# The second projection of a gated recurrence and a shared feed-forward net: one level of Strassen's form against two

## The chip, the cores and the metric

The kernel runs on one core of one Trainium2 chip. The metric is the device time of one execution in microseconds (us). Three runs of the kernel before gave 4150.46, 4151.88 and 4153.29 us, so a median of 4151.88 us. Everything is in 32-bit floats.

## What is computed

The input x is 8 sequences of 1024 tokens with 512 features. The reference, cut to its core:

```python
xn = layernorm(x)
proj = xn @ W1 + b1                        # 512 -> 3 * 1024: hidden, forget, input
hidden, f, i = split(proj, 3)
h = scan of a gated recurrence over the tokens of a sequence
s = h @ W2 + b2                            # 1024 -> 512
shared = (silu(xn @ sgate) * (xn @ sup)) @ sdown      # 512 -> 1024 -> 512
routed = the same with one of 32 experts per token (arg max of xn @ gate_w)
out = x + s * silu(shared + routed)
```

The change concerns the two products with 1024 rows of weights: h @ W2 and the shared net's product with sdown.

## The kernel before

The 8192 tokens are cut into 16 chunks of 512. The work of a chunk is 20 *jobs*: a job makes 256 columns of one of the five first products (hidden, forget, input, gate, up). Each job is a product in Strassen's form: 7 outer products in place of 8 (`multiply`, matmuls at L918), each of them two matmuls of 128 x 128 weights on 256 columns. The trace shows every float matmul as two records, so such an outer product is four records. The program is written out as *slots*, 7 to a job and 140 to a chunk (`SC`). In each slot there is one outer product of a job; `ORDER` fixes which. Work on other engines is put into the slots with `at(slot, ...)`. Each engine then runs its instructions in the order in which the program issues them; within a slot that is first the outer product and its eviction (L932, L934, on ACT), then the steps put there by `at`, then the fill, of which below.

The evictions of a job are joined by adds (L944) one slot later, on DVE, and one of the seven on POOL. A `Cell` (from L948) turns forget, input and hidden of two blocks of 128 rows into the recurrence: a chain of activations on ACT and of tensor operations on DVE at fixed slots after the job's first slot g, among them the two logarithms at g+29 and g+31 (L992, ACT), the difference at g+32 (L996, DVE), two more at g+33 and g+34 (L1000, L1004), and the scans at g+45 and g+47 (L1029). There are four Cells in a chunk, with g at slots 0, 21, 56 and 91. A `Prep` normalizes the next chunk (`normal`, L619) and asks the router; a few of its results go through the PSUM bank that `work` gives out.

The second products of chunk c run in the slots of chunk c+1, as a *fill*: `project_out` is a generator, and `due` says how many of its steps are to be issued by each slot. A chunk has two *units*, half 0 (h @ W2) in slots 1 to 62 and half 1 (the shared net) in slots 63 to 136. A unit is again one product in Strassen's form: 7 outer products `UNIT`, each of 8 matmuls (L1240) of 128 x 128 on 256 columns; a fill step is one matmul, 56 to a unit. Sums of blocks on the left (`out_combine`, L1183) are made on POOL and DVE beforehand; the right sides, 512 KB each, are read from HBM one outer product at a time by `out_fetch` (L1159 to L1164) into three buffers (`wo`). Two PSUM banks (`ps_u`) hold the outer products; each is read out once, 512 elements a partition (L1220, L1223, L1252, L1258, L1263), and the results go to HBM in two stores (L1204). All these transfers are issued on SP's queue, beside the weights of the jobs (L742), their kept sums (L804) and the traffic of `Prep`.

PSUM's eight banks: three for the jobs' chains (`ps_b`), two for their side products (`ps_x`), two for the fill (`ps_u`), and one for `work`.

After the last chunk's slots (END) the rest of the fill runs alone, and then 32 experts are worked through (L308 to L520) with the tokens gathered by a table that `Dispatch` builds during the last chunks; an expert's products are in Strassen's form too (L398), with 118 to 174 columns to a matmul.

Of the kernel before, what the change touches and what calls it, by code (L numbers as in the profile page):

```python
# [34 lines left out]
def tile_kernel(  # L35
# [73 lines left out]
    def work(name):  # L109
        return pools["work"].tile([P, 512], FP, tag="w", name=name)  # L110
# [16 lines left out]
    def iota(name, n, step, base, cm=0):  # L127
        tf = const.tile([P, n], FP, name=name)

        def fill():  # L130
            ti = const.tile([P, n], I32, name=name + "_i", tag="iota_i")
            nc.gpsimd.iota(ti, pattern=[[step, n]], base=base, channel_multiplier=cm)
            nc.vector.tensor_copy(tf, ti)

        later.append(fill)
        return tf
# [446 lines left out]
    class Prep:  # L583
# [127 lines left out]
        def plan(self, g):  # L711
# [15 lines left out]
            at(g + 66, self.router)  # L727
            at(g + 72, self.logits)
            at(g + 76, self.choose)
# [21 lines left out]
    vrow = const.tile([4 * NJ, P], FP, name="vrow")  # L751
# [5 lines left out]
    def zero_rows():  # L757
# [3 lines left out]
        zrow = op.tile([1, H], FP, tag="ea", name="zrow")  # L761
# [119 lines left out]
    def multiply(name, n):  # L881
# [64 lines left out]
        if name == "P2":  # L946
            evict(part("a", 2), None)
# [8 lines left out]
        elif name == "P7":  # L956
            evict(part("u3", 2), 1)
            join(nc.gpsimd if c else nc.vector, o[:, 1, HT:], "u3", "p5")
        elif name == "P4":
            evict(o[:, 1, :HT], 1)  # L960
            natural.pop(n)
# [6 lines left out]
    class Cell:  # L968
# [53 lines left out]
        def scan(self, s):  # L1022
            c, p = self.c, self.p
            j = 2 * p + s
            if s == 0:
                rnn_h[c, p] = hp.tile([P, 2, T], FP, tag="r", name=f"h{c}_{p}", bufs=5)
# [58 lines left out]
    UNIT = ("P1", "P2", "P6", "P5", "P7", "P3", "P4")  # L1085
# [14 lines left out]
    def out_load(half, k, m):  # L1100

        tag, bufs = (("r", 5), ("s", 6))[half]
# [34 lines left out]
    out_w, out_s = {}, {}  # L1137
    far_turn = iter(range(2 * len(UNIT)))
    out_next = iter([(u, name) for u in units for name in UNIT])

    def out_fetch():

        u, name = next(out_next, (None, None))
        if u is None:
            return
        half = u[1]
        if "far" in pools:
            turn = next(far_turn)
            if turn % 5 < 2:
                o = pools["far"].tile([P, NP, HC], FP, tag="far", name=f"far{turn}")  # L1150
            else:
                o = out_tile(f"w{name}_{half}")
            out_w[u, name] = o
        else:
            o = out_w[u, name] = out_tile(f"w{name}_{half}")
# [9 lines left out]

    HALF = 2 * P
# [5 lines left out]
    def out_combine(c, half, q, p):  # L1172
        if p == 0:
            out_s[q] = op.tile([P, NP, HALF], FP, tag=f"s{q}", name=f"s{q}_{c}_{half}")
        A11, A12, A21, A22 = out_part(c, half, p)
        o = out_s[q][:, p, :]
        eng, l, r, op_ = {
            1: lambda: (nc.gpsimd, A21, A22, ALU.add),
            2: lambda: (nc.vector, out_s[1][:, p, :], A11, ALU.subtract),
            3: lambda: (nc.gpsimd, A11, A21, ALU.subtract),  # L1180
            4: lambda: (nc.vector, A12, out_s[2][:, p, :], ALU.subtract),
# [3 lines left out]
    for c in range(NCHUNK):  # L1185
        g = SC * (c + 1)
        fast = c == NCHUNK - 1
        for p in range(NP):
            for q in range(1, 5):
                if p == NP - 1:  # L1190
                    slot = (1, 2, 4, 6)[q - 1]
                else:
                    slot = (110, 112, 122, 132)[q - 1] + p - SC
                at(g + slot, out_combine, c, 0, q, p)
                if fast:
                    slot = (20, 22, 26, 30)[q - 1] + p // 2
                else:
                    slot = (42, 44, 52, 61)[q - 1] + p
                at(g + slot, out_combine, c, 1, q, p)

    def out_store(c, half, m, o):
        i = (c * NT + 2 * m) * P
        rows = rec2[i : i + 2 * P, half * H : (half + 1) * H]
        nc.sync.dma_start(out=rows.rearrange("(q p) f -> p q f", p=P), in_=o)  # L1204

    def project_out():

        for n, u in enumerate(units):
            c, half = u

            chain, side = (
                ps_u.tile([P, 2, HC], FP, tag=f"u{(n + k) % 2}", name=f"u{k}_{n}")
                for k in range(2)
            )
            o = [op.tile([P, 2, H], FP, tag=f"o{m}", name=f"o{half}_{c}_{m}") for m in range(2)]
            part = {}

            def copy(o, ps, m):
                if half:
                    nc.scalar.copy(o, ps)  # L1220
                else:
                    bias = b2b[:, m * HC : (m + 1) * HC].unsqueeze(1).to_broadcast([P, 2, HC])
                    nc.vector.tensor_tensor(o, ps, bias, ALU.add)  # L1223

            def evict(name, ps, m):
                t = part[name] = op.tile([P, 2, HC], FP, tag="e" + name[0], name=f"{name}_{n}")
                copy(t, ps, m)

            for name in UNIT:
                w = out_w.pop((u, name))  # L1230
                if half:
                    w = w.rearrange("p q (m a r) -> p q a m r", m=KH, r=BL)
                ps = side if name in ("P2", "P5", "P3") else chain
                for q in range(2):
                    for p in range(NP):
                        if name in ("P1", "P2", "P4"):
                            lhs = out_part(c, half, p)[{"P1": 0, "P2": 1, "P4": 3}[name]]
                        else:
                            lhs = out_s[{"P5": 1, "P6": 2, "P7": 3, "P3": 4}[name]][:, p, :]
                        nc.tensor.matmul(  # L1240
                            ps[:, q, :], lhsT=lhs[:, q * P : (q + 1) * P], rhs=w[:, p],

                            start=(q == 0 and p == 0 and name in ("P1", "P2", "P5")),
                            stop=(p == NP - 1),

                            skip_group_check=True,
                        )
                        if q == 1 and p == NP - 1:
                            if name == "P1":
                                evict("a1", ps, 0)  # L1250
                            elif name == "P2":
                                nc.vector.tensor_tensor(o[0][:, :, :HC], ps, part["a1"], ALU.add)  # L1252
                            elif name == "P6":
                                evict("a2", ps, 1)
                            elif name == "P5":
                                evict("b5", ps, 1)
                            elif name == "P7":
                                nc.scalar.copy(o[1][:, :, HC:], ps)  # L1258
                                nc.gpsimd.tensor_tensor(
                                    o[1][:, :, HC:], o[1][:, :, HC:], part["b5"], ALU.add  # L1260
                                )
                            elif name == "P3":
                                nc.vector.tensor_tensor(o[0][:, :, HC:], ps, part["a2"], ALU.add)  # L1263
                                at(now + 2, out_store, c, half, 0, o[0])
                            else:
                                copy(o[1][:, :, :HC], ps, 0)
                                at(now + 2, out_store, c, half, 1, o[1])
                            out_fetch()
                        yield

    class Dispatch:
# [16 lines left out]
        def ranks(self, q):  # L1288
# [22 lines left out]
            for _ in range(9):  # L1311
                yield
            ps = work(f"bef{q}")
# [492 lines left out]
```

## Time and profile before

The profiled execution took 4152.99 us; its span from the first to the last instruction is 4151.0 us. Busy time of the engines by stretches of the span:

| stretch, us | what runs | PE | ACT | DVE | POOL | DMA share | GB/s |
|---|---|---|---|---|---|---|---|
| 0 to 163 | chunk 0's jobs, no fill | 134.78 | 103.65 | 111.96 | 85.71 | 0.76 | 252 |
| 163 to 334 | jobs of chunk 1, fill of chunk 0 | 171.00 | 113.14 | 96.36 | 32.38 | 0.72 | 231 |
| 334 to 2564 | jobs of chunks 2 to 14, fill of chunks 1 to 13 | 2230.00 | 1476.17 | 1206.31 | 448.79 | 0.67 | 214 |
| 2564 to 2734 | jobs of chunk 15, fill of chunk 14 | 168.85 | 112.82 | 90.10 | 102.20 | 0.60 | 183 |
| 2734 to 2790 | fill of chunk 15 | 54.63 | 7.46 | 24.92 | 15.69 | 0.77 | 256 |
| 2790 to 4151 | the experts | 1339.84 | 300.79 | 725.95 | 707.73 | 0.77 | 225 |

PE is the matrix engine TensorE, ACT ScalarE, DVE VectorE, POOL GpSimd, SP SyncE. A column of an engine is the time in which it was busy; the DMA share is the mean busy share of the 16 DMA engines. Matmuls overlap, so a record's duration (379 ns for 256 columns) is longer than the distance from its start to the next one's, which is what a stream of matmuls costs. The granted clock of PE is 0.997 of full speed over the whole span.

### The profile page before, as it was taken

Reading aid. Unit: us, or ns where it says so; the run is one execution under the profiler, and the core shown is the slowest. Engines: PE = TensorE matmul, PEld = TensorE weight load, DVE = VectorE, ACT = ScalarE, POOL = GpSimd, SP = SyncE. Lnnn points to the kernel's source line nnn. Section 1 sums busy time; section 2 is a strip of 40 time slices with the busy share of each in tenths; the row PEclk is TensorE's granted clock in tenths of the full one; section 3 lists DMA queues with packets and bytes.
Section 4 is the critical chain, followed back from the end, with each engine's and each line's share of the span. In section 5 each row is a group of like instructions: output and inputs, shape, how many; then the busy total and the mean of one; then the engine's idle time right before and its main releaser. Section 6 shows DMA issues by size and latency. Waiting matters only on the chain. (4 is left out here: it accounts for less than half of the span.)

```text
span 4151.0 us, 60142 instructions
## 1 busy us (share of the span) xinstructions
PE 4099.1 (99%) x21515; PEld 3634.4 (88%) x21515; DVE 2255.6 (54%) x3682; ACT 2114.0 (51%) x4031; POOL 1392.5 (34%) x1539
## 2 busy tenths in 40 slices
PE   7999999999999999999999999999999999999997
PEld 5788888888888888888888888887899999999997
DVE  6655555564555645556455566534555656666631
ACT  5666666666666667666676666731222222222210
POOL 5322111221112211212112122634555555555542
PEclk9999999999999999999999999999999999999999
DMA  8776666666666766667666665666778787887884
GB/s 277 238 221 221 210 221 204 216 224 212 219 206 213 228 214 218 211 198 229 220 218 214 202 223 180 186 221 199 211 228 233 220 244 231 247 252 233 244 262 116
DMA packets 557537, 909.30 MB, mean 219 GB/s; under 512 B 55404, under 2 KB 315404, under 8 KB 556980
## 3 DMA queue, kind: packets, MB, share of 16 engines
q1 hardware_dynamic: 508228, 812.03, 60.9%
q0 software_dynamic: 46880, 89.20, 8.9%
q8 instruction: 172, 2.82, 0.3%
q10 hardware_dynamic: 2128, 4.19, 0.3%
q14 instruction: 129, 1.06, 0.1%
HBM read 786.82 MB, written 136.37 MB: 222 GB/s over the span
## 5 line engine op out<-in xcount | busy, mean ns | idle before, releaser
L918 PE MATMUL b<-t,sums 128*128 128x256 f32 x2536 | 653.9, 380 | 13.3 <-ACT u L932 6.9
L1240 PE MATMUL u<-wP,s 128*128 128x256 f32 x2032 | 596.1, 379 | 0.6 <-ACT a L1220 0.6
L918 PEld LDWEIGHTS b<-t,sums 128*128 128x128 f32 x2536 | 480.8, 190 | 83.1 <-ACT u L932 8.5
L332 PE MATMUL acc<-e_h,e_wd 128*128 128x284 f32 (+26 forms) x2048 | 514.7, 394 | 0.0
L1240 PEld LDWEIGHTS u<-wP,s 128*128 128x128 f32 x2032 | 385.7, 190 | 55.0 <-issue 1.9
L332 PEld LDWEIGHTS acc<-e_h,e_wd 128*128 128x128 f32 x2048 | 373.6, 190 | 64.9
L918 PE MATMUL b<-t,nat 128*128 128x256 f32 x1268 | 325.9, 379 | 5.5 <-ACT u L932 4.7
L253 POOL DMA_INDIRECT e_xs<-rec,fours x276 | 300.2, 1088 | 91.1 <-issue 87.4
L918 PE MATMUL a<-xnT,nat 128*128 128x256 f32 x1268 | 326.3, 380 | 0.0
L918 PE MATMUL c<-xnT,sums 128*128 128x256 f32 x1268 | 325.6, 379 | 0.0
L918 PE MATMUL b<-xnT,nat 128*128 128x256 f32 x1268 | 325.4, 379 | 0.0
L918 PE MATMUL c<-t,sums 128*128 128x256 f32 x1268 | 325.4, 379 | 0.0
L934 ACT ACTIVATE u<-b,vec 128x256 f32<-128x256 f32 x378 | 179.8, 476 | 188.0 <-PE b L918 171.9
L918 PEld LDWEIGHTS b<-t,nat 128*128 128x128 f32 x1268 | 240.5, 190 | 40.0 <-ACT u L932 6.3
L918 PEld LDWEIGHTS a<-xnT,nat 128*128 128x128 f32 x1268 | 241.4, 190 | 33.0
L918 PEld LDWEIGHTS c<-xnT,sums 128*128 128x128 f32 x1268 | 241.3, 190 | 33.0
L918 PEld LDWEIGHTS b<-xnT,nat 128*128 128x128 f32 x1268 | 240.9, 190 | 33.2 <-issue 0.5
L918 PEld LDWEIGHTS c<-t,sums 128*128 128x128 f32 x1268 | 240.9, 190 | 32.8
L1240 PE MATMUL u<-wP,h 128*128 128x256 f32 x768 | 225.2, 379 | 0.0
L996 DVE TENSOR_TENSOR d<-d,m 128x1024 f32<-128x1024 f32 x64 | 87.7, 1370 | 239.8 <-ACT m L992 239.8
L1240 PE MATMUL u<-wP,sh 128*128 128x256 f32 x720 | 215.6, 381 | 0.0
L407 ACT COPY e_s<-e_b 128x284 f32<-128x284 f32 (+21 forms) x216 | 84.4, 391 | 238.6 <-PE e_b L398 238.6
(291 smaller groups left out, 7794.1 us busy)
## 6 DMA issues: line engine op xcount, KB each, us to landing
sums<-sdram SPq DMA_DIRECT2D x300, 512.0 KB, 4.8
nat<-in_L_attn_W_dram SPq DMA_DIRECT2D x192, 512.0 KB, 4.7
wP<-tdram SPq DMA_DIRECT2D x127, 512.0 KB, 4.0
e_w<-L_ffn_routed_gate_w_dram SPq DMA_DIRECT2D x126, 512.0 KB, 4.6
e_w<-n_L_ffn_routed_up_w_dram SPq DMA_DIRECT2D x126, 512.0 KB, 8.1
e_wd<-L_ffn_routed_down_w_dram SPq DMA_DIRECT2D x31, 2048.0 KB, 11.0
nat<-L_ffn_shared_gate_w_dram SPq DMA_DIRECT2D x64, 512.0 KB, 4.9
nat<-n_L_ffn_shared_up_w_dram SPq DMA_DIRECT2D x64, 512.0 KB, 4.4
```

Of the source, the lines that this page charges most:

```text
L253: nc.gpsimd.indirect_dma_start(out=self.xs[t][:, b, :], out_offset=None, in_=rec1.rearrange("n (a d) -> (n a) d", a=NA), in_offset=bass.In ...
L332: nc.tensor.matmul(accs[m][:, :W], lhsT=self.wd[:, j, m * P : (m + 1) * P], rhs=h[:, :W], start=(j == 0), stop=(j == NI - 1),)
L407: nc.scalar.copy(o[:, :W], ps[:, :W])
L918: nc.tensor.matmul(ps, lhsT=lhs[:, k, :], rhs=rhs[:, k, :], start=(new and k == 0), stop=(k == KQ - 1),  skip_group_check=True,)
L934: nc.scalar.activation(o, ps, AF.Identity, bias=bias(n, block))
L996: nc.vector.tensor_tensor(d, d, self.li, ALU.subtract)
L1240: nc.tensor.matmul(ps[:, q, :], lhsT=lhs[:, q * P : (q + 1) * P], rhs=w[:, p],  start=(q == 0 and p == 0 and name in ("P1", "P2", "P5")), ...
```

## The change

For chunks 1 to 14 (`deep`) each of the 7 outer products of a unit is itself made in Strassen's form: 7 inner products (`INNER`) of two matmuls each, 128 x 128 on 128 columns, where there were 8 matmuls on 256 columns. A fill step is now one inner product, 49 to a unit. Inner product i of outer product b stands at step 7b + 3i, so that three outer products are in work at any time, each in a PSUM bank of its own; the third bank is the one that `work` had, and `work` now borrows a bank of `ps_x` in the last slot of a job, to which its users are moved (`aligned`, the router's slots). In a bank, inner P1, P6, P7 and P4 follow each other in the first 128 columns, P2 has the next 128, and P5 and P3 the third.

Four inner products are copied out (ACT, or DVE where the bias is added), three are added to such a copy on DVE one slot later; when an outer product is complete, `out_add` sums the outer products on DVE. The sums of inner blocks on the left are made on POOL (`inner_sum`). The right sides of the inner products are made once, in chunk 0's units, which still run with one level: POOL makes the four sums of an outer product (`out_make`), ACT copies three raw blocks (`out_raw`), and both are written to HBM in pieces of 128 KB. From then on the pieces are read back, four to a buffer, one inner product to a piece.

The order of `UNIT`, the slots of `out_combine`, and some buffers change with it: the jobs' eviction tiles a and u3 have one buffer in place of two, h has four in place of five, results are stored in four quarters of a unit, and some tiles at the start share a buffer. Chunks 0 and 15 keep one level.

```diff
     def work(name):
-        return pools["work"].tile([P, 512], FP, tag="w", name=name)
+        if now < SC:
+            return pools["work"].tile([P, 512], FP, tag="w", name=name)
+        assert now % 7 == 6
+        return ps_x.tile([P, 512], FP, tag=f"x{(now // 7 + 1) % 2}", name=name)
+
+    def aligned():
+        while now % 7 != 6:
+            yield
...
-            at(g + 66, self.router)
-            at(g + 72, self.logits)
-            at(g + 76, self.choose)
+            at(g + 69, self.router)
+            at(g + 76, self.logits)
+            at(g + 77, self.choose)
...
-            evict(part("a", 2), None)
+            evict(part("a", 1), None)
...
-            evict(part("u3", 2), 1)
+            evict(part("u3", 1), 1)
...
-                rnn_h[c, p] = hp.tile([P, 2, T], FP, tag="r", name=f"h{c}_{p}", bufs=5)
+                rnn_h[c, p] = hp.tile([P, 2, T], FP, tag="r", name=f"h{c}_{p}", bufs=4)
...
+    HQ = HC // 2
+    UNIT = ("P1", "P2", "P4", "P6", "P5", "P3", "P7")
+    INNER = ("P1", "P2", "P5", "P6", "P3", "P7", "P4")
...
+    ALL = [(c, half, name) for c, half in units for name in UNIT]
+
+    def deep(b):
+        return 0 < ALL[b][0] < NCHUNK - 1
+
+    LAST = max(b for b in range(len(ALL)) if deep(b))
+    inner_of = {}
+    for b in range(len(ALL)):
+        if deep(b):
+            for i, name in enumerate(INNER):
+                inner_of[7 * b + 3 * i] = (b, name)
...
+    FAR = 3
...
+    def groups(piece):
+        piece = [s for s in piece if s in inner_of]
+        for k in range(0, len(piece), 4):
+            yield ("pieces", piece[k : k + 4])
...
+        if kind == "pieces":
+            o = o.rearrange("p q f -> p (q f)").rearrange("p (s f) -> p s f", s=4)
+            for k, step in enumerate(what):
+                b, name = inner_of[step]
+                out_w[step] = o[:, k, :].rearrange("p (q f) -> p q f", q=2)
+                nc.sync.dma_start(
+                    out=o[:, k, :], in_=tdram2[ALL[b][1:]][:, INNER.index(name), :]
+                )
+            return
...
+        for o, l, r in (
+            (t[:, 0], B12, B11), (t[:, 1], B22, t[:, 0]), (t[:, 3], B21, t[:, 1]),
+            (t[:, 2], B22, B12),
+        ):
+            nc.gpsimd.tensor_tensor(o, l, r, ALU.subtract)
...
+        for k, i in enumerate(("P5", "P6", "P7", "P4")):
+            nc.sync.dma_start(out=d[:, INNER.index(i), :], in_=made[:, k, :])
...
+            r = jp.tile([P, 2, KH, BL], FP, tag=f"i{i[1]}", name=f"raw{b}{i}", bufs=1)
+            nc.scalar.copy(r, quarter(w, half, k, n))
+            at(now + 2, lambda r=r, i=i: nc.sync.dma_start(
+                out=tdram2[half, name][:, INNER.index(i), :], in_=r.rearrange("p q m r -> p (q m r)"),
+            ))
...
-                if p == NP - 1:
-                    slot = (1, 2, 4, 6)[q - 1]
-                else:
-                    slot = (110, 112, 122, 132)[q - 1] + p - SC
+                ends = p == NP - 1
+                slot = {
+                    1: 1 if ends else 134 + p - SC, 2: 2 if ends else 137 + p - SC,
+                    4: 8 + p, 3: 13 + p // 2 if fast else 18 + p,
+                }[q]
                 at(g + slot, out_combine, c, 0, q, p)
                 if fast:
-                    slot = (20, 22, 26, 30)[q - 1] + p // 2
+                    slot = (24, 26, 31, 28)[q - 1] + p // 2
                 else:
-                    slot = (42, 44, 52, 61)[q - 1] + p
+                    slot = (62, 66, 82, 72)[q - 1] + p
...
+        if half or name not in ("P2", "P4", "P5"):
+            nc.scalar.copy(o, ps)
+            return
+        first += HC * (name == "P5")
+        bias = b2b[:, first : first + n]
+        if reps:
+            bias = bias.unsqueeze(1).to_broadcast([P, reps, n])
+        nc.vector.tensor_tensor(o, ps, bias, ALU.add)
...
+    def out_bank_of(b):
+        n = b % 3
+        if n == 2:
+            return pools["work"].tile([P, 512], FP, tag="w", name=f"u{b}")
+        return ps_u.tile([P, 2, HC], FP, tag=f"u{n}", name=f"u{b}").rearrange("p q f -> p (q f)")
...
+        if name == "P2":
+            add(o(0, 0), R)
+            at(now + 2, out_store, b, 0, 0)
+        elif name == "P6":
+            add(R, out_r[b])
+        elif name == "P3":
+            add(o(0, 1), o(1, 1))
+            add(o(0, 1), R)
+            at(now + 2, out_store, b, 0, 1)
+        elif name == "P7":
+            add(R, out_r[b])
+            for n in (1, 0):
+                add(o(1, n), R)
+                at(now + 2, out_store, b, 1, n)
...
+    def inner_sum(b, q):
+
+        o = inner[b, q] = jp.tile([P, 2, P], FP, tag=f"i{q}", name=f"i{q}_{b}", bufs=1)
+        A11, A12, A21, A22 = (inner_block(b, m, k) for m in range(2) for k in range(2))
...
+        l, r, what = {
+            1: lambda: (A21, A22, ALU.add), 2: lambda: (made(1), A11, ALU.subtract),
+            3: lambda: (A11, A21, ALU.subtract), 4: lambda: (A12, made(2), ALU.subtract),
+        }[q]()
+        for o, l, r in zip(parts, l, r):
+            nc.gpsimd.tensor_tensor(o, l, r, what)
...
+        b, name = inner_of[step]
+        if name == "P1":
+            out_bank[b] = out_bank_of(b)
+        n = {"P2": 1, "P5": 2, "P3": 2}.get(name, 0)
+        ps = out_bank[b][:, n * P : (n + 1) * P]
+        w = out_w.pop(step)
+        for i, lhs in enumerate(inner_lhs(b, name)):
+            nc.tensor.matmul(
+                ps, lhsT=lhs, rhs=w[:, i, :], start=(name == "P1" and i == 0), stop=(i == 1),
+                skip_group_check=True,
+            )
+        o = {"P2": (0, 0), "P3": (0, 1), "P4": (1, 0), "P7": (1, 1)}.get(name)
+        o = o and target(b)[:, o[0], o[1] * HQ : (o[1] + 1) * HQ]
+        side = {"P2": "P1", "P3": "P6", "P7": "P5"}.get(name)
+        if side:
+            kept = inner.pop((b, side))
+            at(now + 1, lambda: nc.vector.tensor_tensor(o, ps, kept, ALU.add))
+        elif name == "P4":
+            out_copy(b, o, ps, 0, HQ)
+            at(now + 2, out_add, b)
+        else:
+            e = inner[b, name] = jp.tile(
+                [P, HQ], FP, tag="e" + name, name=f"e{name}_{b}", bufs=1 + (name == "P5")
+            )
+            out_copy(b, e, ps, 0 if name == "P1" else HQ, HQ)
...
+        def step(s):
+            if s in inner_of:
+                inner_product(s)
+                used[0] += 1
+                if used[0] % 4 == 0 or s == left[-1]:
+                    out_fetch()
+
+        for b, (c, half, name) in enumerate(ALL):
+            if deep(b):
+                for k in range(7):
+                    step(7 * b + k)
+                    if k % 3 == 0 and k < 9:
+                        inner_sum(b, (1, 2, 4)[k // 3])
+                    if k == 2 and deep(b - 1):
+                        inner_sum(b - 1, 3)
+                    yield
+                continue
...
-    PER = len(UNIT) * NP * 2
+    PER = [7 * 7 if deep(7 * u) else 7 * 2 * NP for u in range(len(units))]
+    PER[-2] += len([s for s in inner_of if s >= 7 * LAST + 7])
+    TOTAL = sum(PER)
...
+        before, (a, b) = sum(PER[: 2 * (c - 1)]), PER[2 * (c - 1) : 2 * c]
         if c == NCHUNK:
-            return int(2 * (c - 1) * PER + min(max(RATE * s, 0), 2 * PER))
-        part = min(max(s / 62, 0), 1) + min(max((s - 62) / 74, 0), 1)
-        return int((2 * (c - 1) + part) * PER)
+            return int(before + min(max(RATE * s, 0), a + b))
+        return int(before + min(max(s / 62, 0), 1) * a + min(max((s - 62) / 74, 0), 1) * b)
```

## The prediction, made before the run

> **What bounds the kernel now.** I read the head of the page first, then busy times by stretches, then the order of time on PE, DVE and ACT in one chunk, the seventh (its first slot starts at 1021.39 us).
>
> ```profile
> span 4151.0 us, 60142 instructions
> PE 4099.1 (99%) x21515; PEld 3634.4 (88%) x21515; DVE 2255.6 (54%) x3682; ACT 2114.0 (51%) x4031; POOL 1392.5 (34%) x1539
> ...
> L918 PE MATMUL b<-t,sums 128*128 128x256 f32 x2536 | 653.9, 380 | 13.3 <-ACT u L932 6.9
> L1240 PE MATMUL u<-wP,s 128*128 128x256 f32 x2032 | 596.1, 379 | 0.6 <-ACT a L1220 0.6
> ```
>
> 99% alone says little, since records overlap. The stretches say more:
>
> ```profile
> core 0: us, PE busy (x) PEld busy (x) DVE busy (x) ACT busy (x) POOL busy (x), PEclk, DMA share, GB/s
> 1021.39:1192.61 171.22, 171.22 (x795) 149.02 (x794) 94.41 (x157) 112.20 (x203) 35.06 (x39) 1.00 0.67 214
> 1192.61:1363.40 170.79, 170.79 (x797) 149.37 (x797) 90.80 (x131) 113.49 (x205) 34.00 (x39) 1.00 0.67 215
> ```
>
> In a middle chunk PE never pauses, at full clock, while ACT has 34% free, DVE 46%, POOL 80%, DMA a third. So only PE's own stream sets the length, and an idle microsecond put into it is paid in full. That stream in order of time (start, us, engine, line):
>
> ```profile
> 1059.38 1.03 PE L918 MATMUL b<-t,sums 128*128 128x256 f32 x4
> 1060.24 0.59 PE L1240 MATMUL u<-wP,s 128*128 128x256 f32 x2
> 1060.67 1.03 PE L918 MATMUL a<-xnT,nat 128*128 128x256 f32 x4
> ```
>
> From 1059.38 to 1060.67 lie 6 records, 216 ns each (that is the distance of their starts; 379 ns is one's duration). A chunk has 140 x 4 job records and 112 x 2 fill records: 784 x 0.216 = 169.3 us, plus the router's.
>
> **What the shorter matmuls cost.** The trace has the shape asked for: the expert with 256 tokens, one row per outer product.
>
> ```profile
> 3671.90 1.05 PE L398 MATMUL e_b<-e_xsT,e_w 128*128 128x128 f32 x8
> 3672.79 1.06 PE L398 MATMUL e_c<-e_ts,e_w 128*128 128x128 f32 x8
> 3673.68 1.06 PE L398 MATMUL e_a<-e_xsT,e_w 128*128 128x128 f32 x8
> 3674.58 1.06 PE L398 MATMUL e_b<-e_ts,e_sm 128*128 128x128 f32 x8
> 3675.47 0.82 PE L332 MATMUL acc<-e_h,e_wd 128*128 128x260 f32 x3
> ```
>
> 32 records in 3.57 us: 111.6 ns each, of the same 128 x 128 weights that load in 190 ns. Half of 216 is 108, so shortness costs 3%. An outer product goes from 16 x 216 = 3.456 us to 28 x 111.6 = 3.125 us. There are 14 chunks x 14 = 196 of them: 677.4 us become 612.5, **64.9 us saved**. Bounds: at 112 ns 62.7 saved; at the 109 ns between the router's transposes (L679, 128 columns) 79.
>
> The Trainium skill speaks against such matmuls: "TensorE: Matmul & The Clock Gate", section "Back-to-back issue gap", gives about 81 ns sustained for 128 columns against 131 for 512, so some 98 for 256 by a straight line, an estimate. By that ratio the inner products would cost 677.4 x 7/8 x (81 x 2/98) = 980 us, 300 more than now; the rows of this trace show no such floor at 128 columns, and the sum goes by them.
>
> **What is added beside PE, per chunk.** Prices are straight lines through rows: ACT 128x512 out of PSUM 0.58 us (L1220, L1258), 128x256 0.37 (L932), so 128x128 0.27; DVE 0.69 and 0.42 (L1223, L944), so 0.28; POOL 1.275 (L1259) and 0.86 (L1183, L944), so 0.65.
> - ACT: half 1 copies 28 inner products, half 0 16 (the other 12 go to DVE with the bias): 44 x 0.27 = 11.9, less 6 x 0.58: +8.4, to 121 of the new 166.
> - DVE: 42 adds and 12 copies x 0.28 = 15.1, 14 adds of `out_add` x 0.69 = 9.7, less 8 x 0.69: +19, to 112 of 166.
> - POOL: per chunk 48 sums of 128 elements x 0.65 and 32 of 256 x 0.86 = 58.7, less 2.5: +56, to 91 of 166. Lower bound of a short sum 0.43 (half of 0.86): +46.
> - SP: one issue holds it 0.46 us (364 in chunks 6 to 9). 98 pieces for 14 fetches and 8 stores for 4: +88, 40 us on top of 41, to 82 of 166.
>
> All lies beside PE on average. On the path is only what PE waits for: a bank's earlier read-out, sums on the left, pieces.
>
> **New waits.** An inner P4 writes over the columns that P7 left, 3 steps later; in between DVE must have added P7, one slot after it. A slot of half 0 lasts 4 x 0.216 + 0.79 x 4 x 0.1116 = 1.22 us (1.25 now). So DVE may lag some 3 slots. It does, where a Cell stands in its queue:
>
> ```profile
> 1058.03 0.54 DVE L619 TENSOR_SCALAR x<-x,mv,rs 128x512 f32<-128x512 f32 x1
> 1062.89 1.23 DVE L996 TENSOR_TENSOR d<-d,m 128x1024 f32<-128x1024 f32 x1 [4.33 <-ACT m L992]
> 1064.15 1.23 DVE L1000 SCALAR_TENSOR_TENSOR d<-i,d 128x1024 f32<-128x1024 f32 x1
> 1065.30 0.42 DVE L944 TENSOR_TENSOR i<-a,p 128x256 f32<-128x256 f32 x1
> ```
>
> L996 belongs to slot 32, which starts at 1060.67, and is held by ACT's logarithm until 1062.89. By `due`, step 22 (a P7) is issued in slot 31, its add in slot 32 right behind L996, and step 25 (that product's P4) in slot 34. The add would end at 1064.15 + 0.28, 3.8 us into slot 32; PE wants it at 2 x 1.22 + 0.86 = 3.3 us. That is 0.5 us; two more copies on ACT ahead of the logarithm (0.27 each) make it **1.0**. At the second Cell (L996 issued in slot 53) the queue is emptied at 1096.40, 9.4 us after that slot's start; four inner adds or copies come in (1.1; the L1263 that goes pays for one of `out_add`) and the add of slot 58 itself, 10.8, against P4 in slot 61 at 8 x 1.22 + 0.86 = 10.6: 0.2, and with DVE and POOL longer in each other's way (L996 there took 1.56 for 1.23) **0.5**. The third misses by 0.1, and ACT's read-out of a job's P5 there (done 0.6 us before P3 needs the bank) gets two copies ahead of it: **0.3** in all. The fourth loses a long copy for two short: 0. Sum 1.8 us a chunk, x 14 = **25 us**; bounds 0 (ACT's and DVE's slack elsewhere absorbs it) and double, 50.
>
> Left sums have 6 steps, 9 us, against bursts of 4 sums (3.4 to 5.2 us) on a POOL at 55%, so nothing. The borrowed bank is asked for three slots on, 3.6 us, and read in 0.7: nothing, unless DVE lags as above (0.7 a chunk, in the bounds).
>
> **Pieces.** Each is asked for 8 steps ahead (two buffers of four stand before it): 12.3 us, less 1.8 to issue four and 4 to 5 to land (wP 4.0, a 128 KB load 4.1), leaves 5.5. Bytes rise by 5.5 MB a chunk, 33 GB/s; in time, packets of 1 KB took 53 ns and of 4 KB 203, so the share goes from 0.67 to about 0.80. I take nothing.
> The skill warns here too: "DMA: Bandwidth & Descriptors", section "Bandwidth", asks for 1 MiB to reach 75% of peak and has 138 GB/s at 64 KB. An estimate of 200 GB/s at 128 KB from its two rows would add 0.27 us to each piece, 26 us of DMA time a chunk, share 0.96; this trace shows landing times alone, no rate of single pieces.
>
> **Other stages.** Chunk 1's jobs get the making of the pieces: ACT +42 x 0.37 = 15.5, POOL 56 x 0.86 = 48, both below 80%: 2 us (0 to 8). Chunk 0 already waits for ACT (11.6 us on L932); single buffers for a and u3 may add: 1 us (0 to 4). `Dispatch` gets 5 slots longer, ending at slot 2257; the table is wanted at 2259, so 0, and past that 1.2 us a slot.
>
> **Sum.** -64.9 + 25 + 2 + 1 = -37 on a run of 4152.99 (span 4151.0 and 2 around it): 4116; that run was 1.1 above the median, so **4115**. Its own range: 4090 to 4140.
>
> **Rivals.**
> 1. *No new wait worth counting.* ACT's logarithms come no later and the lags overlap. For it: 34% free ACT; against: the 0.5 us of the first Cell. -64.9 + 1: 4088, **4087** against the median. Chance 0.25.
> 2. *DMA becomes the bound.* Slots 0 to 20, about 40 to 50 and 60 to 70 already run near the most that any slice shows (278):
>
> ```profile
> 1021.39:1046.00 24.61, 24.61 (x116) 21.66 (x115) 14.50 (x23) 9.73 (x23) 5.58 (x5) 1.00 0.83 275
> 1071.00:1084.00 13.00, 13.00 (x62) 11.42 (x62) 9.40 (x14) 10.18 (x19) 7.24 (x8) 1.00 0.92 278
> 1096.00:1109.00 13.00, 13.00 (x65) 10.46 (x64) 10.34 (x17) 8.29 (x16) 1.58 (x2) 1.00 0.88 278
> ```
>
> Half 0 asks for 49 x 131 KB in 75.5 us, 85 GB/s for 47 now. If 278 is the ceiling, the backlog grows by 24.6 x 35/278 = 3.1 us, then 1.8 and 1.5: 6.4 a chunk, 90 in all, -65 + 90 + 3: **4180**, slower. It decides once a backlog passes the 5.5 us spare; single stretches stay below, hence chance 0.17.
> 3. *The queues eat the gain.* 4.5 us of waits a chunk (Cells, borrowed bank, left sums behind POOL): **4150**. Against it: it needs over twice my sum. Chance 0.11.
> 4. *The form isn't faster at all*: if alternating with long matmuls the short ones cost the 190 ns of a weight load, 5488 x 0.19 = 1043: 4517. The L398 rows speak against it. Chance 0.04.
>
> **How the numbers follow.** Forecast 0.43. Range 4084 to 4165: from just under rival 1 over rival 3, leaving most of rival 2, rival 4 and a little at the bottom out. This kernel's runs differ by 0.07%, so 0.2% (8 us) is told from no change. Faster 0.43 + 0.25 + 0.03 = 0.71; same 0.05, slower 0.17 + 0.04 + 0.03 = 0.24, from rival 3 in parts.
>
> **What would show it.** Right: 128-column records 112 ns apart beside 216; middle chunks of 168 us; PE's waits for DVE's add after P7 near slots 34 and 61, 1 to 2 us a chunk; ACT near 73%, DVE 67%, POOL 55%, DMA 0.80. Chunks of 166 us without waits are rival 1; PE waiting for pieces is rival 2; PE waiting for POOL's sums or the borrowed bank is rival 3. I am wrong in the main if a stretch of middle chunks is over 170.8 us.

## The result, and the profile after

The changed kernel takes **4224.36 us** (median of four runs, 4223.72 to 4229.39) against 4151.78 us before: a ratio of 1.0177, interval 1.016 to 1.0195. It is 1.8% slower; 0.9% faster was forecast.

The head of its page answers to the first lines shown of before:

```profile
span 4222.9 us, 71000 instructions
...
PE 4067.9 (96%) x23867; PEld 3649.0 (86%) x23867; DVE 2655.1 (63%) x4540; ACT 2212.9 (52%) x4615; POOL 2266.2 (54%) x2683
...
L1406 PE MATMUL u<-w_pieces,i 128*128 128x128 f32 x3136 | 483.0, 277 | 35.4 <-issue 33.9
```

PE's share has fallen from 99% to 96%, and the inner matmuls (L1406; lines have moved, so L918 is now L925, L932 is L939, L944 is L951, L996 is L1003, L1000 is L1007, L1029 is L1036, L1223 is L1330) have idle time ahead of them. One middle chunk by stretches (us, then busy time of PE, PEld, DVE, ACT and POOL, clock, DMA share, GB/s):

```profile
1557.30:1731.70 174.40, 168.02 (x966) 150.12 (x966) 116.62 (x193) 119.48 (x242) 93.75 (x118) 1.00 0.77 241
```

It lasts 174.4 us where it lasted 170.8. PE is idle for 6.4 of them, with DVE, ACT and POOL below 70% and the clock full. So no engine is the bound: PE waits for single instructions.

**Where the time went.** I added up the distances from each matmul record's start to the next one's, and split them into what the record's columns cost at full clock (216 ns for 256 columns, 112 for 128) and the rest, which is waiting (a record slowed by the clock after a wait is in the rest too).

| us | before | after | difference |
|---|---|---|---|
| records of the fill | 773.6 (3584 long) | 96.7 (448 long) + 609.8 (5488 short) | -67.1 |
| waits in chunk 0's stage | 33.9 | 34.6 | +0.7 |
| waits in chunk 1's jobs | 0.3 | 2.0 | +1.7 |
| waits in the 12 stages after (fill of chunks 1 to 12) | 3.5 | 99.9 | +96.4 |
| waits in the last two stages (fill of chunks 13, 14) | 2.8 | 31.1 | +28.3 |
| waits in what is left | 2.7 | 11.4 | +8.7 |

-67 and +136 give +69; the spans differ by 71.9, so some 3 us stay unplaced. The gain came as forecast, and the waits took twice as much. Whom PE waits for, over the whole span (us in total, times, longest us):

```profile
PE u L1406 <- DVE o L1415: 40.2, 28, 6.6
PE u L1406 <- issue: 33.9, 44, 1.4
PE u L1406 <- DVE R L1415: 23.0, 13, 1.8
PE b L925 <- ACT u L939: 11.5, 7, 4.3
```

The fourth line is chunk 0's, and was there before. The other three are new. L1415 is the add of P2, P3 or P7 to its kept copy, on DVE. The `issue` line is mostly the same wait with another name, as the second example below shows.

**Six waits a chunk.** In the chunk shown, PE waits before steps 4 (1.30 us), 25 (1.33), 27 (0.47), 43 (1.59), 67 (1.99) and 92 (0.66). PE around step 25, the one that the prediction followed at the first `Cell` (start, us, then in brackets the idle time before):

```profile
1601.64 1.03 PE L925 MATMUL c<-xnT,sums 128*128 128x256 f32 x4
1603.84 0.71 PE L1406 MATMUL u<-w_pieces,h 128*128 128x128 f32 x4 [1.17 <-DVE o L1415]
```

And DVE:

```profile
1602.36 1.23 DVE L1003 TENSOR_TENSOR d<-d,m 128x1024 f32<-128x1024 f32 x1 [4.70 <-ACT m L999]
1603.51 0.28 DVE L1415 TENSOR_TENSOR o<-u,eP 128x128 f32<-128x128 f32 x1
```

The add stands behind L1003, which ACT's logarithm (L999) let go only at 1602.36, after 4.70 us in which DVE did nothing; PE goes on 0.05 us after the add. This is the mechanism of the prediction. Step 43, at the second `Cell`, is another matter. DVE first:

```profile
1629.11 1.50 DVE L1003 TENSOR_TENSOR d<-d,m 128x1024 f32<-128x1024 f32 x1 [2.60 <-ACT m L999]
1630.53 1.10 DVE L645 STREAM_TRANSPOSE xnT<-xq 128x512 f32<-128x512 f32 x1
1631.55 1.19 DVE L1007 SCALAR_TENSOR_TENSOR d<-i,d 128x1024 f32<-128x1024 f32 x1
1632.65 0.69 DVE L1344 TENSOR_TENSOR R<-R,T 128x512 f32<-128x512 f32 x1
1633.25 0.42 DVE L951 TENSOR_TENSOR u<-a,p 128x256 f32<-128x256 f32 x1
1633.59 0.29 DVE L1415 TENSOR_TENSOR o<-u,eP 128x128 f32<-128x128 f32 x1
```

Then PE:

```profile
1633.98 0.68 PE L1406 MATMUL u<-w_pieces,i 128*128 128x128 f32 x4 [1.43 <-issue]
```

Step 43 is a P7; it writes the bank's first 128 columns. The add that ends at 1633.88 reads P3, in the third 128. PE waits for it all the same, and steps 27 (a P5, for P2's add) and 92 (a P7, for P3's) do so too. (These three also need a sum that POOL makes; at step 43 POOL's last one had ended by 1631.20, and one of the experiments takes POOL out of the question.) The program's list of waits says why: every inner product waits for the engine that last read its **bank**, whatever the columns. The Trainium skill asks for just that in "PSUM — Partial Sum Buffer", section "PSUM bank collisions raise a hardware error": to guard by bank and quarter of the partitions, not by address. These three waits agree with it, in that the program guards by bank; what an unguarded matmul would do, no run here shows. So seven products of a bank, three steps apart, make a chain in which each must be read before the next, and a late DVE can miss any of the three adds in it. The prediction had looked at one, P7's.

**DVE's own work grew by more than the new instructions.** Sums of durations per middle chunk: DVE 98.9 us before, 129.4 after, +30.5 for the +19 foreseen. Instructions that the change does not touch grew from about 93.2 to 101.8 us. Another 3.1 us are in the 14 adds of `out_add` (L1344), which took 0.91 us each where 0.69 was set. Three of the costlier groups of DVE between 500 and 2200 us (busy us, mean ns of one):

```profile
L1036 DVE TENSOR_TENSOR_SCAN h<-i,carry,f 128x512 f32<-128x512 f32 x40 | 63.2, 1580 | 0.2
...
L1007 DVE SCALAR_TENSOR_TENSOR d<-i,d 128x1024 f32<-128x1024 f32 x38 | 56.7, 1491 | 0.0
...
L1415 DVE TENSOR_TENSOR T<-u,eP 128x128 f32<-128x128 f32 x117 | 32.7, 279 | 28.7 <-PE u L1406 28.7
```

Before, L1007 (then L1000) took:

```profile
L1000 DVE SCALAR_TENSOR_TENSOR d<-i,d 128x1024 f32<-128x1024 f32 x39 | 47.2, 1211 | 0.7
```

The scan took 1326 ns before. L1415, with one operand in PSUM, took the 0.28 us that was estimated. POOL had gone from 35.1 to 96.2 us a chunk.

**The last two stages.** `Dispatch` builds the experts' table there with many small DVE instructions, now 5 slots later. On DVE, from 2619.70 us, 21 of them (about 0.2 us each) and six longer operations stand ahead of an inner add that ends at 2627.89. PE meanwhile:

```profile
2620.34 1.03 PE L925 MATMUL b<-t,nat 128*128 128x256 f32 x4
2627.95 1.23 PE L1406 MATMUL u<-w_pieces,s 128*128 128x128 f32 x4 [6.58 <-DVE o L1415]
2628.97 1.91 PE L925 MATMUL c<-t,sums 128*128 128x256 f32 x4
```

After that wait the four long records take 1.70 us to the next group's start instead of 0.86: 427 ns apart. The granted clock fell with it, to a mean of 0.64 over these 11.5 us:

```profile
2620.50:2632.00 11.50, 4.92 (x18) 4.01 (x18) 11.09 (x32) 1.08 (x4) 4.44 (x5) 0.64 0.41 126
```

### The profile page after: what moved, and what is told of

Same layout as the page of the kernel before. It is cut to its first block, busy times and chain, and to the rows that moved or that the text cites. A ratio compares the mean times of both kernels' runs of the same rounds, so it can differ in the third digit from the quotient of the medians.

```text
span 4222.9 us, 71000 instructions
## 1 busy us (share of the span) xinstructions
PE 4067.9 (96%) x23867; PEld 3649.0 (86%) x23867; DVE 2655.1 (63%) x4540; ACT 2212.9 (52%) x4615; POOL 2266.2 (54%) x2683
## 5 line engine op out<-in xcount | busy, mean ns | idle before, releaser
L925 PE MATMUL b<-t,sums 128*128 128x256 f32 x2536 | 656.2, 381 | 11.5 <-ACT u L939 5.7
L1406 PEld LDWEIGHTS u<-w_pieces,i 128*128 128x128 f32 x3136 | 470.0, 192 | 94.9 <-issue 55.2
L1406 PE MATMUL u<-w_pieces,i 128*128 128x128 f32 x3136 | 483.0, 277 | 35.4 <-issue 33.9
L925 PEld LDWEIGHTS b<-t,sums 128*128 128x128 f32 x2536 | 454.5, 191 | 61.3 <-ACT u L941 7.0
L339 PEld LDWEIGHTS acc<-e_h,e_wd 128*128 128x128 f32 x2048 | 373.6, 190 | 64.9
L925 PE MATMUL b<-t,nat 128*128 128x256 f32 x1268 | 326.5, 380 | 6.6 <-ACT u L939 5.8
L925 PE MATMUL c<-t,sums 128*128 128x256 f32 x1268 | 327.7, 381 | 2.7 <-DVE ovexp L1639 2.3
L925 PE MATMUL c<-xnT,sums 128*128 128x256 f32 x1268 | 326.3, 380 | 1.9 <-issue 1.2
L925 PE MATMUL b<-xnT,nat 128*128 128x256 f32 x1268 | 327.2, 381 | 0.0
L925 PE MATMUL a<-xnT,nat 128*128 128x256 f32 x1268 | 327.1, 381 | 0.0
L302 POOL COPY pin<-e_h 1x1 f32<-1x1 f32 x148 | 37.4, 253 | 475.7 <-DVE e_h L447 345.1
L1388 POOL TENSOR_TENSOR i<-s 128x256 f32<-128x256 f32 x224 | 206.5, 922 | 149.1 <-PE u L1406 147.6
L925 PEld LDWEIGHTS b<-xnT,nat 128*128 128x128 f32 x1268 | 224.9, 191 | 34.5 <-DMA w_pieces<-d_P 8.4
L925 PEld LDWEIGHTS b<-t,nat 128*128 128x128 f32 x1268 | 226.5, 191 | 32.2 <-ACT u L939 7.2
L925 PEld LDWEIGHTS c<-xnT,sums 128*128 128x128 f32 x1268 | 226.4, 191 | 25.2 <-issue 1.4
L925 PEld LDWEIGHTS c<-t,sums 128*128 128x128 f32 x1268 | 225.6, 191 | 25.4 <-DVE ovexp L1639 2.5
L925 PEld LDWEIGHTS a<-xnT,nat 128*128 128x128 f32 x1268 | 226.0, 191 | 22.3
L1406 PEld LDWEIGHTS u<-w_pieces,s 128*128 128x128 f32 x1344 | 202.3, 192 | 47.0 <-DVE o L1415 29.8
L1406 PE MATMUL u<-w_pieces,s 128*128 128x128 f32 x1344 | 206.8, 277 | 23.9 <-DVE o L1415 23.9
```

Source lines behind the costliest of these rows:

```text
L302: nc.gpsimd.tensor_copy(pin, self.mark)
L339: nc.tensor.matmul(accs[m][:, :W], lhsT=self.wd[:, j, m * P : (m + 1) * P], rhs=h[:, :W], start=(j == 0), stop=(j == NI - 1),)
L925: nc.tensor.matmul(ps, lhsT=lhs[:, k, :], rhs=rhs[:, k, :], start=(new and k == 0), stop=(k == KQ - 1),  skip_group_check=True,)
L1388: nc.gpsimd.tensor_tensor(o, l, r, what)
L1406: nc.tensor.matmul(ps, lhsT=lhs, rhs=w[:, i, :], start=(name == "P1" and i == 0), stop=(i == 1), skip_group_check=True,)
```

## The experiments

The theory: PE waits because DVE's adds come late for a bank that the next product needs, by their slot and by the order of DVE's queue, which POOL's load makes worse. The rivals: the waits are for pieces of the weights; the sums on POOL are late themselves; contention costs PE time in some other way. Single runs stand beside a run of before on the same chip (4152 or 4153 us).

**The adds in the matmul's own slot.**

```diff
-            at(now + 1, lambda: nc.vector.tensor_tensor(o, ps, kept, ALU.add))
+            nc.vector.tensor_tensor(o, ps, kept, ALU.add)
```

> Edit: the add of inner P2, P3 and P7 is issued on DVE in the slot of its matmuls and not one slot later. Theory Q (PE waits because DVE's queue reaches these adds late, and the next inner product in the same bank, three steps on, may not start before): each add moves ahead of what DVE has to do in the slot between, so each wait shortens by up to a slot (1.2 us). The six waits of a middle chunk (1.30, 1.33, 0.47, 1.59, 1.99, 0.66 us) would be some 1.5 us together in place of 7.3, so about 80 us less over 14 chunks: 4145 us. Theory D (the 128 KB pieces, SP's issues or DMA): no change, 4224. Theory C (DVE is late only because POOL's sums hold its operands): the waits shrink too, so it isn't told from Q here.

Measured: 4183.38 us, a middle chunk 170.5. That is 41 us off the changed kernel, not the 79 expected. Waits in the 12 middle stages fell from 99.9 to 54.3 us; the wait at step 4 grew to 1.72 us, and the last two stages kept 29.9 us. The slot matters and is about half of the middle stages' waits.

**ACT reads the bank instead of DVE.**

```diff
-            at(now + 1, lambda: nc.vector.tensor_tensor(o, ps, kept, ALU.add))
+            nc.scalar.copy(o, ps)
+            at(now + 1, lambda: nc.vector.tensor_tensor(o, o, kept, ALU.add))
```

> Edit: inner P2, P3 and P7 are copied out of PSUM by ACT at once, and DVE adds the kept copy to that from SBUF one slot later, so no bank waits for DVE any more (but for the bias copies). Theory Q: PE's waits on DVE's adds are gone, some 7.3 us a chunk; ACT gets 42 copies a chunk more (0.27 us each, 11 us, to 86% of a chunk) and may hold PE for 1 to 2 us a chunk at the Cells' activations: 4224 - 100 + 20 = about 4140, between 4115 and 4165. Theory D: 4224 or more. Theory C: DVE's operations stay as long as they are, and the time falls as by Q, since what is late no longer holds a bank.

Measured: 4206.85 us, a middle chunk 173.2: a miss. Its waits of PE:

```profile
PE c L925 <- DVE lgT L694: 22.3, 14, 1.8
PE u L1406 <- DVE o L1330: 20.5, 13, 1.6
PE b L925 <- DVE t L837: 13.8, 9, 5.2
```

The waits for L1415 are gone from the list's head, and other readers on DVE stand in their place: the router's reduction in the borrowed bank (L694), the copies that add the bias (L1330), the sums that a job's matmuls take (L837). The added operands in SBUF took DVE from 129.4 to 137.5 us a chunk and the copies ACT from 132.9 to 147.4. PE here waits for a late DVE at the next places where the two meet.

**POOL's left sums made once.** `inner_sum` reuses one tile for each q, so the products that use these sums are not the reference's.

```diff
+        if q in once:
+            inner[b, q] = once[q]
+            return
-        o = inner[b, q] = jp.tile(
+        o = inner[b, q] = once[q] = jp.tile(
```

> Edit: the sums of inner blocks on the left (POOL) are made once only and then used over and over, so POOL does about as much as in the kernel before, and the products of the sums are not the reference's. Theory C: DVE's operations take what they took before the change (L1036 1.34 and not 1.55 us, L1007 1.21 and not 1.49), DVE is in time, and PE's waits all but vanish: about 4115. Theory Q without contention: waits as before, 4224. Both in part, which I hold likeliest: the waits fall to a half, about 4170.

Measured: 4168.73 us, a middle chunk 170.7, as expected. POOL fell to 33.5 us a chunk and DVE to 119.3; the scan's mean is 1386 ns, L1007's 1208, near what they were before. Three of the six waits are left (1.33, 1.28, 1.46, at the first three Cells). The second of them, in a middle chunk, is step 43 again:

```profile
1436.55 0.71 PE L1409 MATMUL u<-w_pieces,i 128*128 128x128 f32 x4 [1.11 <-DVE o L1418]
```

Its weights are a sum made long before, so it cannot wait for POOL, and it is put down to DVE's add (L1418 is L1415 of the changed kernel) that reads other columns of its bank. POOL's load is behind 56 us of the loss, though little waiting for POOL itself shows: PE 1.3 us in the whole changed kernel, DVE none and ACT 6.6 us in ten middle chunks.

**Both.**

> Edit: the adds in the slot of their matmuls (as in e1_same_slot) and no sums of inner blocks on POOL but the first (as in e3_no_left_sums, so the products of the sums are not the reference's). e1 took 41 us off, e3 54. If late DVE adds are all that holds PE, and POOL's sums and the place in DVE's queue both feed that lateness, the two together leave hardly a wait: a middle chunk of 166.2 to 167 us, 4224 - 105 = about 4120 in all with the waits of the last two chunks still in it. If something else (weight pieces, ACT, the borrowed bank) lies just under the DVE waits, the chunk stays near 170 us.

Measured: 4113.31 us. Two middle chunks:

```profile
666.00:833.00 167.00, 167.00 (x967) 150.79 (x967) 107.77 (x197) 119.06 (x245) 33.71 (x37) 1.00 0.80 255
834.00:1000.00 166.00, 166.00 (x961) 149.84 (x960) 106.17 (x192) 118.36 (x242) 33.71 (x37) 1.00 0.81 254
```

PE is busy throughout, and 9.0 us of waits are left in the 12 middle stages. The two causes nearly add up: 41 + 56 is 97 of the 111 us gained, and in a middle chunk 3.8 + 3.6 of 7.6. This run, which leaves out POOL's left sums, is what the change would be worth with most of its waits removed: -40 us.

**Before, with POOL's load alone.** The kernel before, with 56 sums of 256 elements a chunk added on POOL, which nothing reads:

```diff
+                        if 0 < c < NCHUNK - 1 and p % 2 == 0:
+                            hs = (rnn_h, ffn_h)[half][c, p]
+                            spare = jp.tile([P, 2 * P], FP, tag="spare",
...
+                            nc.gpsimd.tensor_tensor(spare, hs[:, 0, : 2 * P], hs[:, 1, : 2 * P], ALU.add)
```

> Edit: the kernel before, with one added sum of 256 elements on POOL beside every fourth matmul of the second products of chunks 1 to 14, results unused: 56 a chunk, nearly 50 us of POOL. Theory C in its general form (a busy POOL makes DVE's operations on two SBUF operands longer): DVE's time in a middle chunk grows from 98.9 us by 5 to 10. Theory Q: that alone costs no time, since before the change no bank waits for DVE within three steps: 4152 within 8 us. If a busy POOL cost PE time by itself, it would be over 4160.

Measured: 4159.46 us, 6 over before and within the 8 allowed. DVE's sum went from 98.9 to 116.4 us a chunk (5 to 10 were expected), the same row as above:

```profile
L1000 DVE SCALAR_TENSOR_TENSOR d<-i,d 128x1024 f32<-128x1024 f32 x39 | 62.5, 1602 | 0.7
```

Yet PE never paused in a middle chunk:

```profile
677.00:848.00 171.00, 171.00 (x798) 149.70 (x798) 107.92 (x137) 113.05 (x204) 91.91 (x96) 1.00 0.67 216
```

So POOL lengthens DVE's work in both kernels, and in a middle chunk of the kernel before, where no product waits for DVE within three steps, that costs no time. The 6 us lie in the last two stages, where the waits of matmuls grew by about as much: one of 2.2 us, whose releaser the profile does not show, and smaller ones for ACT and DVE. That excludes contention by itself as the cause of the middle chunks' loss.

**Pieces in one transfer.** Four pieces come as one transfer of 512 KB, some of them the wrong ones:

```diff
-                nc.sync.dma_start(
-                    out=o[:, k, :], in_=tdram2[ALL[b][1:]][:, INNER.index(name), :]
-                )
+            nc.sync.dma_start(
+                out=o[:, : len(what), :], in_=tdram2[ALL[b][1:]][:, : len(what), :]
+            )
```

> Edit: the four pieces of a buffer are fetched by one transfer of 512 KB (four neighbours of one outer product, so not the right weights), the same bytes in a quarter of the issues and in packets of 4 KB. Theory D: SP and the DMA engines are relieved, and the waits fall, 4224 down to 4150 or less. Theories Q and C: no wait of PE hangs on a piece, so within 10 us of 4224.

Measured: 4229.91 us, a middle chunk 174.3, the same six waits. The pieces are not what PE waits for.

**The adds two slots later** (the changed kernel with `now + 2`; at the very end the last inner products are read after later ones went into the bank, so those results differ).

> Edit: the changed kernel with the adds of inner P2, P3 and P7 issued two slots after their matmuls, not one: the opposite of e1. Theory Q: the margin of three slots or so shrinks by one, each of the six waits grows by up to 1.2 us, and adds that were just in time become late too: 6 to 14 us a chunk more, 4224 + 85 to 190 = 4310 to 4410. Theories C and D alone: no change.

Measured: 4325.09 us, as expected, a middle chunk 181.3, waits of 185 us in the 12 middle stages, single ones 2.7, 2.3 and 3.1 us long. One slot each way: -41 and +101. The lateness of these adds sets the length, and it costs more than in proportion. Part of that is the clock: of the 36 waits of 2.3, 2.7 and 3.1 us in these stages 24 were followed by records at half the pace, as after the long wait shown above, for some 1.7 us each or 3.4 us a chunk. Why the other 12 were not, these runs do not show.

**Mending it: sums moved.** The adds as in the first experiment, half 0's left sums on DVE moved off the crowded slots 5 to 9, and chunk 14 left at one level (with it goes a line that counts the fill's steps):

```diff
-                    1: 1 if ends else 134 + p - SC, 2: 2 if ends else 137 + p - SC,
-                    4: 8 + p, 3: 13 + p // 2 if fast else 18 + p,
+                    1: 1 if ends else 134 + p - SC, 2: 2 + p if fast else 12 + 2 * p,
+                    4: 8 + p if fast else 20 + 2 * p, 3: 13 + p // 2 if fast else 18 + p,
...
-        return 0 < ALL[b][0] < NCHUNK - 1
+        return 0 < ALL[b][0] <= 13
```

> Edit: adds in the slot of their matmuls; half 0's left sums that DVE makes moved from slots -3 to 2 and 8 to 11 to slots 12 to 18 and 20 to 26; chunk 14 with one level, so two levels in chunks 1 to 13 only. Theory Q: e1's wait of 1.7 us at slot 8 goes, a middle chunk takes 168.5 to 169 us in place of 170.5, and the last stage is as before the change: 4125 to 4135, faster than the kernel before by 20 us.

Measured: 4137.30 us, 2 over the range, a middle chunk 168.3. The wait at step 4 is gone; 0.58 and 0.56 us are left at the first Cell. The last two stages still take 178.8 and 179.0 us.

**The same with chunk 13 left at one level too** (`<= 12`).

> Edit: as f1_moved, but two levels in chunks 1 to 12 only, so that no inner product runs beside the making of the tables in chunks 14 and 15. f1 had its last two stages at 178.8 and 179.0 us against 174.3 and 170.8 before the change. Theory Q (DVE, filled by the tables' small operations there, reaches the adds late): both stages return to their old length, -12 us, less a chunk's gain of 2: 4127, between 4122 and 4132. If these stages are long for another reason, 4139.

Measured: 4133.92 us (4133.23 to 4139.42), ratio 0.9958 (0.9942 to 0.9973): a miss by 7 us. The last two stages still take 177.7 and 175.8 us. The first has the six inner products that are left over from chunk 12 (24 short records, 2.7 us), which the expectation did not count; the second has none, and this wait:

```profile
2558.51 2.05 PE L925 MATMUL b<-t,sums 128*128 128x256 f32 x4 [3.59 <-DVE t L837]
```

A job's matmul waits for a sum on DVE that stands behind `Dispatch`'s small instructions, and the records after it run at half the pace. In the kernel before, where `Dispatch` is not aligned, the longest wait for such a sum (L830) was 1.0 us. So moving `Dispatch` by `aligned` probably has a price of its own; no run moves it alone.

**The next chunk's normalization earlier by 6 or 8 slots**, to thin out DVE's queue at the first Cell:

```diff
-                at(g + 16 + 2 * t, self.stats, t)
-                at(g + 32 + 2 * t, self.normal, t)
+                at(g + 10 + 2 * t, self.stats, t)
+                at(g + 24 + 2 * t, self.normal, t)
...
-            at(g + 24, self.variance, 0, NT)
-            at(g + 28, self.spread, 0, NT)
+            at(g + 18, self.variance, 0, NT)
+            at(g + 20, self.spread, 0, NT)
```

> Edit: as f2_to12, and the next chunk's statistics, normalizing and what stands between moved some 6 to 8 slots forward, out of the first Cell's place in DVE's queue (slots 32 to 38) into slots where DVE waits. Theory Q: the last two waits of a middle chunk (0.6 us each at slots 38 to 41) shrink, up to 1 us a chunk: 4127 - 8 = about 4119, no slower than f2 in any case.

Measured: 4125.01 us (4124.79 to 4125.12), ratio 0.9934 (0.9911 to 0.9956). That is 8.9 us less than the run before it, as expected, and 6 above 4119, because that run was 7 above its own forecast. Again, in more rounds:

> The kernel of f3_early again, for its interval against the kernel before: 4125 us within 3, a ratio of 0.9935 within 0.0015, if its 27 us are the shorter matmuls' gain less the waits that its trace shows. Were they an accident of one chip or build, it would be back near 4152.

Measured: 4124.30 us (4122.62 to 4126.32) against 4152.46, ratio 0.9934 (0.9921 to 0.9948). A middle chunk of it:

```profile
676.00:844.00 168.00, 167.79 (x966) 150.08 (x966) 120.62 (x198) 118.47 (x243) 96.90 (x117) 1.00 0.81 254
```

Its fill records take 716.0 us, 57.6 less than before (12 chunks have the new form); waits, counted as in the table, are 69.1 us for 43.2. This version beats both kernels, by 28 us the one before and by 100 us the change.

## Why the prediction was wrong

**Right.** The gain: 64.9 us from short records 111.6 ns apart; measured 67.1. The 980 us that the prediction estimated from the Trainium skill's figures ("TensorE: Matmul & The Clock Gate", section "Back-to-back issue gap") did not come: these records took 609.8 us. The loads: ACT 121, DVE 112 and POOL 91 us busy and a DMA share of 0.80 were forecast for a middle chunk; 119.5, 116.6, 93.8 and 0.77 were measured (busy time, in which overlaps count once; DVE's sum of durations grew by more, see below). "Pieces: nothing" held, so rival 2 falls with the one-transfer run; rival 4 with the table of records. The first Cell's mechanism was traced rightly, and 1.0 us stood for what were 1.33 and 0.47.

**The step that failed is "New waits", 25 us with an upper bound of 50.** It measured 96 in the 12 middle stages (8.0 a chunk for 1.8), and about 28 more in the last two. Three things in it were wrong:

1. *Which products wait.* It counted only "an inner P4 writes over the columns that P7 left". Three of six waits are for adds whose columns the waiting product does not touch. A bank of seven products has to be followed as one chain, whole. No run was made that waits by columns; this rests on the places of the waits, on the program's lists, and on step 43, which waits 1.28 us for DVE also where POOL makes no left sums.
2. *DVE's prices.* The sum took each duration from a trace in which POOL had 35 us a chunk, and set POOL to 91. Contention stood in it as one late Cell's 1.56 for 1.23 us. DVE's excess was 11.5 us a chunk (30.5 less 19): 8.6 of it in instructions that had not changed, and 3.1 in `out_add`'s adds of two operands in SBUF, priced at 0.69 us from a row that reads PSUM (L1223), where they took 0.91. Taking the left sums off POOL gave back 55.6 us, through DVE's shorter work as far as the waits show; no run parts it from what else POOL hands over sooner.
3. *Where DVE is crowded.* Only the four Cells were looked at. Step 4 (1.30 us) is none: old and new sums and the last unit's `out_add` meet there in slots 5 to 9. Moving the sums removed that wait.

The second, third and fourth Cells (0.5, 0.3 and 0 forecast; 1.59, 1.99 and 0.66 measured) were margins of tenths of a microsecond, the difference of two sums near 10 us. Such a margin says "tight", not "0.2".

**"`Dispatch` ... so 0"** priced only when the table is ready. What its instructions push back on DVE was not asked. Two waits of PE behind them (2.3 and 6.6 us) and the slowed records after the second make some 11 of the last two stages' +28 us; the rest are mostly waits like those of the middle chunks.

**Rival 3**, that the queues eat the gain, was the outcome; it was priced at 4.5 us a chunk, from the same margins, and needed 8 and a tail. The upper end of 4165 came from there. Its 4150 leaves out the 3 us of other stages that rival 2 counts, and rival 1's 4088 and 4087 should be 4089 and 4088; neither slip matters here.

The run with both causes taken out measured 4113.31, 2 us from the forecast of 4115. The gain agrees, and what was mis-sized is what those two edits remove; that it comes so close is luck. It has some 26 us more of waits than the kernel before, near the 28 forecast, but only about 6 of them in the middle stages, and more than half in the last two and behind them.

## What to carry to other kernels

When work on PE is cut into shorter pieces that share a bank, list every reader of the bank in order and give each the time until the next product, however far apart their columns are; an engine that is two thirds busy, as DVE was here, can be late for such dates wherever its queue holds an instruction that waits for another engine. Price the queue's instructions under the load that the other engines will have after the change, not under the one of the trace. And when steps are moved to aligned slots, ask what stands behind them in their queue.

## What the runs showed of the hardware

- With 57 us more of POOL sums a chunk, DVE's work grew by 17.5 us with no instruction added to it: an operation of two operands in SBUF went from 1.21 to 1.60 us, while reads out of PSUM (L1415) kept 0.28 beside a POOL just as busy. The Trainium skill says so in "SBUF — State Buffer", section "Who interferes with whom": a DVE instruction with two inputs in SBUF contends with a POOL instruction that reads there, and one with at most one such input does not, outside the modes that use both ports. The rows agree; the price is theirs.
- The waits of 3.59 and 6.58 us shown above were each followed by long records 427 ns apart instead of 216, for a few microseconds, and so were two thirds of those of 2.3 to 3.1 us in the run with later adds. Such a wait can cost more than it lasts, but does not always: those of 2 us and less in the changed kernel's middle chunks were followed by records at full speed, and so was one of 3.58 us in the last kernel (from 2550.99 to 2551.42 lie two records):

```profile
2550.05 1.10 PE L925 MATMUL b<-t,sums 128*128 128x256 f32 x4 [3.58 <-DVE t L837]
2550.99 0.59 PE L1461 MATMUL u<-w_whole,h 128*128 128x256 f32 x2
2551.42 1.03 PE L925 MATMUL a<-xnT,nat 128*128 128x256 f32 x4
```

- A float matmul record of 128 columns costs 111 to 112 ns also when it alternates with ones of 256.
